# Graph attention with Strassen products on one core: side tasks split at each wait and spaced, the head weights folded with a on TensorE, the last feed-forward steps held as filler

## The chip, the core and the metric

One core of a Trainium2 chip runs the kernel. The metric is device time in microseconds of one execution, the median of several runs. The engines are PE (matmuls and transposes; its weight load PEld overlaps), DVE, ACT, POOL, and SP, which here only issues DMAs.

## The reference, cut to what matters

x is (128, 64, 512) in float32: 128 graphs of 64 nodes that share one adjacency matrix.

```python
h = jnp.maximum(_layernorm(x, axis=-1), 0.0)
def _gat_heads(x, adj, W, a):
    Wh = jnp.einsum('bnf,hfo->bhno', x, W)
    f1 = jnp.einsum('bhno,ho->bhn', Wh, a[:, :O])
    f2 = jnp.einsum('bhno,ho->bhn', Wh, a[:, O:])
    e = f1[:, :, :, None] + f2[:, :, None, :]
    e = jnp.where(e > 0, e, LEAKY_ALPHA * e)
    e = jnp.where(adj[None, None] > 0, e, NEG_INF)
    attn = jax.nn.softmax(e, axis=-1)
    return jnp.einsum('bhnm,bhmo->bhno', attn, Wh)
h = jax.nn.elu(_gat_heads(h, adj, W_heads, a_heads))      # 4 heads
h = jnp.transpose(h, (0, 2, 1, 3)).reshape(B, N, -1)      # 2048 wide
out = jax.nn.elu(_gat_heads(h, adj, W_out[None], a_out[None])[:, 0])
ffn = jnp.maximum(out @ w1 + b1, 0.0) @ w2 + b2
y = ffn + out
x + (y - mu) / jnp.sqrt(var + LN_EPS) * ln_gamma + ln_beta
```

## The kernel before

The 8192 rows are 64 tiles of 128 rows (two graphs each). Four tiles are a group, and there are 16 groups. Five stages make a group's work.

**Stage a** (L374) reads x, normalizes it (`norm1`, L273: BN_STATS on DVE L264, one small power on POOL, `n1nb` on DVE L278, the ReLU to `hn` on ACT L280), transposes `hn` on PE (`pth`, L293), copies it on ACT (`hT`, L295), and multiplies it with the 8 columns of `wa`, the head weights folded with a (`pf`, L300). Softmax 1 (L306, for a pair of tiles) spreads f2 over the diagonal of an identity (`s1dg`, DVE L311), lets PE add it up over the rows (`s1pe`, L318), then adds, masks, takes leaky ReLU, exponential (`s1e`, ACT L329), sum, reciprocal and `s1A` (DVE L343). PE transposes the weights (`s1pt`, L360 to L368) and ACT copies them to `at`.

**attend1** (L396) multiplies the attention weights with `hn` itself, ahead of the head projection (`pz` into `z`). **project1** (`g_a`) multiplies z with the head weights, one head at a time, and `late` work on ACT, DVE and POOL applies elu and forms the sums `hS`, `h` (L434, L435, L472, L499). **project2** (`g_b`) multiplies the 2048-wide result with W_out and gives `wh` (L505, L507).

**Stage e** (L543) is the second attention: the scores `jf` (eight on DVE, L522), `s2dg`, `s2pe`, `s2A`, the transposes `s2pt` (L532), and `pa` (attend2, L538) with elu to `o`. **feed_forward** (L551) transposes `o` (`pto`, L561, to `ot`), does the two products `g_c` and `g_d` with the ReLU `rt` between (ACT L588), and `finish` normalizes (`n2st`, L264; L607, L608), adds x (`xr`) and stores.

Each product of a group with a 512 by 512 weight is done in Strassen-Winograd form: seven products p of 256-wide quadrants in place of eight (`unit`, L182). Sums and differences of the quadrants of the activations are made on POOL or DVE (`sums`, L252 to L255: `zs_z`, `zs_o`, `hS`), those of the results on ACT and DVE (`s_a`, `t_a`, L193, L195). The p-th result goes to one of three banks of the unit, so that the order of p says when each sum is needed. The sums of weights are made once at the start by POOL (`weight_sums`, L139), stored to DRAM (`tc`), and every piece is then streamed from DRAM by SP through a ring of 12 buffers `w` (`piece`, L154).

Order of the work (L624 to L678): in iteration g, project1(g), 24 steps of g_a, carries a side list of stage_e(g-1) (stage_a(1) for g=0), whose entries are spread evenly over the steps. project2(g), 28 steps of g_b, carries attend1(g+1), the transposes, the two products and finish of feed_forward(g-1), and stage_a(g+2). `mix` interleaves lists by their fractions and `run` spreads a side list over steps. An entry that does nothing (`lambda: None`) is a gap. A scheduler then places the instructions on the in-order queue of each engine, so that an instruction that has to wait holds all behind it on its engine. PSUM is six banks for products and two ("aux") for transposes, scores and spreads.

At the start, ACT issues the loads of the weights (`fetch`, buffers `pw`); `fold` (L124) multiplies the head weights with a row of a, broadcast to all rows (`ab`), in 32 DVE operations with accumulation (`jk`, L133); and POOL's weight sums wait for the last of these by a dependency made by hand.

Of the kernel before, what the change touches and what calls it, by code (L numbers as in the profile page):

```python
# [20 lines left out]
def gat_preln_kernel(  # L21
# [38 lines left out]
    G = 4  # L60
# [63 lines left out]
    def fold(m):  # L124

        for c in range(2):
            ab = wk.tile([P, O], FP, tag="elu", name=f"ab{c}_{m}", bufs=3)
            nc.sync.dma_start(
                out=ab, in_=a_heads[m:m + 1, c * O:(c + 1) * O].to_broadcast([P, O])
            )  # L130
            for k in range(KC):
                junk = wk.tile([P, O], FP, tag="t", name=f"jk{c}_{m}_{k}")
                last = nc.vector.scalar_tensor_tensor(  # L133
                    junk, MT[m][:, k, :], 1.0, ab, ALU.mult, ALU.mult,
                    accum_out=wa[:, k, c * H + m:c * H + m + 1],
                )
        return last

    def weight_sums(m):  # L139
# [5 lines left out]
        first = nc.gpsimd.tensor_tensor(s[0][:, 0], b12, b11, ALU.subtract)  # L145
# [6 lines left out]
        return first  # L152
# [133 lines left out]

    def project_f(p):

        hts = []
        for t in (2 * p, 2 * p + 1):  # L290
            pt = aux([P, KC, P], f"pth{t}")
            for k in range(KC):
                nc.tensor.transpose(pt[:, k, :], HN[t][:, ts(k, P)], ident)  # L293
            hT = wk.tile([P, KC, P], FP, tag="hT", name=f"hT{t}")
            nc.scalar.copy(hT, pt)  # L295
            hts.append(hT)
        pf = aux([P, 2, 2 * H], f"pf{p}")
        for j, hT in enumerate(hts):
# [7 lines left out]
    def softmax(f1, f2, q, tag, t):  # L306
# [9 lines left out]
        )  # L316
        pe = aux([P, q, N], f"{tag}pe{t}")
# [15 lines left out]
        nc.vector.reciprocal(r, s)  # L333

# [17 lines left out]

    def attn_weights(p):
        f = FF.pop(p)
        A1[p] = softmax(
            f[:, 0].rearrange("p t h -> p (t h)"), f[:, 1].rearrange("p t h -> p (t h)"),
            2 * H, "s1", p,
        )

    def transpose_weights(p):  # L360
        A = A1.pop(p)
        for j in range(2):
            t = 2 * p + j
            pt = aux([P, H, P], f"s1pt{t}")
            for h in range(H):
                nc.tensor.transpose(pt[:, h, :], A[:, j * H + h].rearrange("p b m -> p (b m)"), ident)
            AT[t] = big.tile([P, H, P], FP, tag="at", name=f"at{t}", bufs=G)
            nc.scalar.copy(AT[t], pt)  # L368
# [255 lines left out]
    for m in range(H):  # L624
        fetch(m)
# [84 lines left out]
```

## Time and profile before

| what | value |
|---|---|
| median of 3 runs | 2600.03 us (2592.85 to 2607.5) |
| the profiled execution's own time | 2600.03 us |
| its span, first to last instruction | 2598.2 us |
| PE busy | 2408.9 us, 93% |
| DVE / ACT / POOL busy | 1495.3 / 775.1 / 1002.8 us |
| mean granted TensorE clock | 0.970 |
| DMA | 371.03 MB, 143 GB/s in the mean |

PE is busy nearly all the time, so the table is read for the rest: what PE waits for, where it runs at a lower clock, and what the first and last hundred microseconds hold in which it is not yet, or no longer, fully fed. One iteration of the loop takes 157.0 us in the middle of the run.

### The profile page before, as it was taken

The page shows a single profiled execution, that of the slowest core. Times are in us where ns is not written, and L with a number is a line of the kernel's source. Part 1 is how long each engine was busy: PE and PEld are TensorE (multiplying, and loading weights), DVE is VectorE, ACT ScalarE, POOL GpSimd, SP SyncE. Part 2 cuts the span into 40 slices and gives each one's busy share as a digit, 9 for nine tenths or more (in the row PEclk, how much of TensorE's full clock was granted, in tenths as well). Part 3 has the DMA queues.
Part 4 walks back from the last instruction along what each step waited for, and adds up shares of the span by engine and source line. Part 5 has one row for each costly group of instructions (what it writes and reads, how often), then busy time and mean ns, then how long its engine had stood idle before and what let it go on. Part 6 is the DMA issues. An engine that isn't in the chain of part 4 may idle for free.

```text
span 2598.2 us, 32561 instructions
## 1 busy us (share of the span) xinstructions
PE 2408.9 (93%) x11552; PEld 2012.8 (77%) x11552; DVE 1495.3 (58%) x2566; ACT 775.1 (30%) x1345; POOL 1002.8 (39%) x851
## 2 busy tenths in 40 slices
PE   1599999999999999999999999999999999899995
PEld 1488787788788887888788788887887878788884
DVE  6565556474654747557465654747556473744645
ACT  0242414224142331414224151331514223141401
POOL 5733422434334343432534333343432434333342
PEclk9899999999999999999999999999999999999998
DMA  8643434344443444435344443444444354434451
GB/s 288 218 130 126 133 124 156 114 159 133 142 135 120 158 132 146 133 120 165 122 159 133 155 131 115 157 133 150 131 129 158 123 161 130 150 125 151 151 165 50
DMA packets 261584, 371.03 MB, mean 143 GB/s; under 512 B 22448, under 2 KB 145328, under 8 KB 261424
## 3 DMA queue, kind: packets, MB, share of 16 engines
q1 hardware_dynamic: 253264, 347.99, 42.0%
q10 hardware_dynamic: 5280, 10.49, 1.2%
q0 software_dynamic: 2880, 10.49, 1.0%
q8 instruction: 93, 1.52, 0.2%
q14 instruction: 67, 0.55, 0.1%
HBM read 341.61 MB, written 27.26 MB: 142 GB/s over the span
## 4 chain that ended last, share of the span: by engine, by line
PE 77%; DVE 15%; issue 3%; DMA 2%; POOL 1%; ACT 1%; SPq 0%; DVEq 0%; POOLq 0%; ACTq 0%
PE g_a L228 27%; PE g_b L243 23%; PE g_d L243 7%; PE g_c L228 6%; PE pz L411 4%; PE pf L300 2%; DVE o L608 2%; DVE jf L522 2%; PE pa L538 2%; PE pzS L411 1%; PE pto L561 1%; DVE s1A L343 1%; DVE n2st L264 1%; PE s1pe L318 1%; DVE o L607 1%
## 5 line engine op out<-in xcount | busy, mean ns | idle before, releaser
L243 PE MATMUL g_b<-w,h 128*128 128x256 f32 x2560 | 603.4, 381 | 0.0
L243 PEld LDWEIGHTS g_b<-w,h 128*128 128x128 f32 x2560 | 477.4, 190 | 78.2 <-issue 14.0
L228 PE MATMUL g_a<-zs_z,w 128*128 128x256 f32 x1536 | 367.6, 388 | 14.5 <-POOL zs_z L253 12.9
L228 PE MATMUL g_a<-z,w 128*128 128x256 f32 x1536 | 374.9, 386 | 0.0
L228 PEld LDWEIGHTS g_a<-zs_z,w 128*128 128x128 f32 x1536 | 299.8, 196 | 65.0 <-POOL zs_z L253 13.3
L228 PEld LDWEIGHTS g_a<-z,w 128*128 128x128 f32 x1536 | 296.8, 193 | 48.9 <-issue 4.4
L243 PE MATMUL g_b<-w,hS 128*128 128x256 f32 x1024 | 264.6, 397 | 0.0
L472 POOL TENSOR_TENSOR hS<-hS,h 128x512 f32<-128x512 f32 x64 | 81.3, 1271 | 401.3 <-DVE hS L435 401.3
L243 PEld LDWEIGHTS g_b<-w,hS 128*128 128x128 f32 x1024 | 190.6, 195 | 41.0 <-issue 11.4
L499 POOL TENSOR_TENSOR h<-h,h 128x512 f32<-128x512 f32 x64 | 85.4, 1336 | 252.3 <-PE g_b L243 252.3
L434 ACT ACTIVATE exc<-exc 128x512 f32<-128x512 f32 x256 | 161.4, 630 | 7.6
L253 POOL TENSOR_TENSOR zs_z<-zS,z 128x512 f32<-128x512 f32 x64 | 89.8, 1404 | 151.4 <-PE g_d L243 83.2
L255 POOL TENSOR_TENSOR zs_z<-z,zs_z 128x512 f32<-128x512 f32 x64 | 81.8, 1278 | 162.4 <-PE g_a L228 145.4
L435 DVE SCALAR_TENSOR_TENSOR h<-exc,h 128x512 f32<-128x512 f32 x128 | 105.7, 831 | 60.2 <-ACT exc L434 60.2
L243 PE MATMUL g_d<-w,rt 128*128 128x256 f32 x512 | 136.5, 415 | 0.7 <-ACT s_d L193 0.7
L243 PEld LDWEIGHTS g_d<-w,rt 128*128 128x128 f32 x512 | 106.5, 210 | 26.1 <-issue 6.2
L499 POOL TENSOR_TENSOR h<-hS,h 128x512 f32<-128x512 f32 x64 | 81.7, 1277 | 108.4 <-PE g_b L243 107.6
L228 PE MATMUL g_c<-ot,w 128*128 128x256 f32 x512 | 121.8, 381 | 0.0
L228 PE MATMUL g_a<-zS,w 128*128 128x256 f32 x512 | 121.1, 379 | 0.0
L599 POOL TENSOR_TENSOR o<-s_d,o 128x512 f32<-128x512 f32 x32 | 41.4, 1294 | 201.6 <-ACT s_d L193 160.0
L588 ACT ACTIVATE rt<-rt,b1s 128x256 f32<-128x256 f32 x96 | 43.5, 500 | 243.0 <-DVE rt L585 243.0
L604 POOL TENSOR_TENSOR xr<-xr,bs 128x512 f32<-128x512 f32 x64 | 85.5, 1337 | 74.3 <-DMA xr<-in_x_dram 51.9
(134 smaller groups left out, 3829.0 us busy)
## 6 DMA issues: line engine op xcount, KB each, us to landing
w<-tc SPq DMA_DIRECT2D x640, 256.0 KB, 2.7
w<-in_L_gnn_W_heads_dram SPq DMA_DIRECT2D x192, 256.0 KB, 2.8
w<-in_L_gnn_W_out_dram SPq DMA_DIRECT2D x192, 256.0 KB, 2.7
w<-in_L_gnn_w_dram SPq DMA_DIRECT2D x96, 256.0 KB, 2.7
x<-in_x_dram SPq DMA_DIRECT2D x66, 256.0 KB, 3.2
xr<-in_x_dram SPq DMA_DIRECT2D x64, 256.0 KB, 3.0
out_dram<-o SPq DMA_DIRECT2D x64, 256.0 KB, 2.2
tc<-pt POOLq DMA_DIRECT2D x20, 512.0 KB, 5.5
```

The costliest lines, as they stand in the source:

```text
L228: nc.tensor.matmul(bk[:, o, :], w[:, k, ts(o, P)], a[:, k, :], start=start and o == 0 and k == 0, stop=k == 1, skip_group_check=True,)
L243: nc.tensor.matmul(bk[:, j, :], a[:, k, ts(j, P)], w[:, k, :], start=start and k == 0 and j == 0, stop=i == len(ms) - 1 and k == 1, skip_g ...
L253: eng.tensor_tensor(s2, s1, a11, ALU.subtract)
L255: eng.tensor_tensor(s3, a22, s2, ALU.subtract)
L300: nc.tensor.matmul(pf[:, j, :], hT[:, k, :], wa[:, k, :], start=(k == 0), stop=(k == KC - 1))
L411: nc.tensor.matmul(banks[b][:, c, :].rearrange("p (h n) -> p h n", h=H), src[rows, off + c * P:off + (c + 1) * P], at[rows, :, rows], star ...
L434: nc.scalar.activation(ex, ex, AF.Exp, scale=-1.0)
L435: nc.vector.scalar_tensor_tensor(dst, ex, -1.0, src, ALU.add, ALU.max)
L472: nc.gpsimd.tensor_tensor(dst, dst, H1["22"][:, h], ALU.add)
L499: nc.gpsimd.tensor_tensor(dst[:, h], x0[:, h], x1[:, h], ALU.subtract)
L522: nc.vector.scalar_tensor_tensor(junk, WH2[g][:, j], 1.0, ao[:, c, :], ALU.mult, ALU.mult, accum_out=f[:, c, j:j + 1],)
L604: nc.gpsimd.tensor_tensor(xr, xr, bs, ALU.add)
```

## The change

Six edits are made.

1. `fold` moves from DVE to PE. a is loaded once (`ah`, 16 KB, in place of eight broadcasts) and transposed; each of the 16 blocks of 128 rows of the head weights is transposed in four parts (`pwt`), copied from PSUM by ACT or DVE in turn (`wT`), and multiplied with two columns of a (`pwa`). POOL's weight sums no longer wait for the fold. The startup runs norms, transposes of hn, fold, then per pair scores and softmax, then the transposes of the weights.
2. The side tasks are split where one engine waits for another: `transpose_h` from `project_f` (with four `hT` buffers in place of two), `spread` from `softmax`, and the scores from softmax 2. stage_a has 15 entries in place of 9 and stage_e 25 in place of 24, with gaps between.
3. The weights of softmax 1 are 512 elements (e times r, heads side by side and the first repeated) in place of a block-diagonal 1024, and `at` is laid out per graph.
4. The order of p in g_d is (1, 6, 5, 2, 3, 7, 4) in place of (1, 2, 6, 5, 7, 3, 4).
5. The first z sums (group 0, head 0) go to DVE in place of POOL.
6. In the last iteration the last seven steps of g_d of group 14 are held out of project2(15) and run with the first 15 entries of stage_e(15). The last feed_forward puts two finishes after step 12 of 14.

```diff
-                last = nc.vector.scalar_tensor_tensor(
-                    junk, MT[m][:, k, :], 1.0, ab, ALU.mult, ALU.mult,
-                    accum_out=wa[:, k, c * H + m:c * H + m + 1],
-                )
+    def fold(m, aT, pw):
+        for k in range(KC):
+            pt = bank(f"pwt{m}_{k}").rearrange("p a b -> p (a b)").rearrange("p (o q) -> p o q", o=KC)
+            for o in range(KC):
+                nc.tensor.transpose(pt[:, o, :], MT[m][:, k, ts(o, P)], ident)
+            wT = wk.tile([P, KC, P], FP, tag="elu", name=f"wT{m}_{k}", bufs=3)
+            if k % 2 == 0:
+                nc.scalar.copy(wT, pt)
+            else:
+                nc.vector.tensor_copy(wT, pt)
+            for o in range(KC):
+                nc.tensor.matmul(
+                    pw[:, k, :, m], wT[:, o, :], aT[:, m, :, o],
...
+    def transpose_h(t):
+        pt = aux([P, KC, P], f"pth{t}")
...
+        HT[t] = wk.tile([P, KC, P], FP, tag="hT", name=f"hT{t}", bufs=4)
+        nc.scalar.copy(HT[t], pt)
...
         return [
-            lambda: norms(p), lambda: project_f(p), lambda: norms(r), lambda: attn_weights(p),
-            lambda: project_f(r), lambda: transpose_weights(p), lambda: attn_weights(r),
+            lambda: norms(p), lambda: norms(r), lambda: transposes(p), lambda: transposes(r),
+            lambda: f(p), lambda: None, lambda: attn_weights(p), lambda: f(r), lambda: None,
+            lambda: attn_weights(r), lambda: None, lambda: transpose_weights(p), lambda: None,
             lambda: None, lambda: transpose_weights(r),
         ]
...
+        eng = nc.vector if (g, h) == (0, 0) else nc.gpsimd
+        sums(eng, z["S1"][:, h], z["11"][:, h], z["12"][:, h], z["22"][:, h], *ZSUM[h])
...
-        return [lambda: softmax2(g)] + wait * 9 + [lambda: transpose_weights2(g)] + wait + [
-            lambda: (attend2(g, 0), attend2(g, 1))] + wait + [lambda: (attend2(g, 2), attend2(g, 3))
-        ] + wait * 8
+            [lambda: scores2(g)] + gap * 6 + [lambda: softmax2(g)] + gap * 6
+            + [lambda: transpose_weights2(g)] + gap * 2 + attend[0:1] + attend[1:2] + gap
+            + attend[2:3] + attend[3:4] + gap * 3
...
-        tail = mix(ff, stage_a(g + 2)) if ff or g + 2 < NG else []
-        run(project2(g), mix(attn, tr) + tail + fin if attn or tr else tail + fin)
-    for fn in stage_e(NG - 1):
+        if g < NG - 1:
...
+        else:
+            held = len(ff) - 7
+            run(project2(g), tr + [lambda: None] * 8 + ff[:held])
+            run(ff[held:] + fin, stage_e(g)[:15])
+    for fn in stage_e(NG - 1)[15:]:
         fn()
-    for fns in feed_forward(NG - 1):
-        run(fns)
+    tr, ff, fin = feed_forward(NG - 1)
+    run(tr + ff[:12] + fin[:2] + ff[12:] + fin[2:])
```

**First place: the head of project1.** PE's queue at the first steps of project1 of group 2, before. `g_a` are the products of head 0 (bank 0) in the order of p that the number in `w` tells, and `s2pe` is the spread of softmax 2 of group 1.

```order
L228 MATMUL g_a_0_2546<-z_2_1882,w_1_2547 128x256 x4
L228 MATMUL g_a_0_2592<-zs_z_0_2540,w_6_2593 128x256 x4
L228 MATMUL g_a_0_2601<-zS_2_1962,w_5_2602 128x256 x4
L228 MATMUL g_a_0_2546<-z_2_1905,w_2_2616 128x256
L318 MATMUL s2pe_2574<-s2dg_2572,blkones 128x256
L228 MATMUL g_a_0_2546<-z_2_1905,w_2_2616 128x256 x3
L228 MATMUL g_a_0_2592<-zs_z_0_2541,w_7_2626 128x256 x4
L228 MATMUL g_a_0_2601<-zs_z_0_2542,w_3_2637 128x256 x4
```

PE after, from the same product on:

```order
L240 MATMUL g_a_0_2642<-z_2_1980,w_1_2643 128x256 x4
L240 MATMUL g_a_0_2670<-zs_z_0_2636,w_6_2671 128x256 x4
L240 MATMUL g_a_0_2679<-zS_2_2053,w_5_2680 128x256 x4
L240 MATMUL g_a_0_2642<-z_2_2003,w_2_2694 128x256 x4
L240 MATMUL g_a_0_2670<-zs_z_0_2637,w_7_2704 128x256 x4
L240 MATMUL g_a_0_2679<-zs_z_0_2638,w_3_2715 128x256 x4
L240 MATMUL g_a_1_2726<-z_2_1980,w_1_2727 128x256 x4
L341 MATMUL s2pe_2735<-s2dg_2668,blkones 128x256
L240 MATMUL g_a_1_2753<-zs_z_1_2688,w_6_2754 128x256 x4
L240 MATMUL g_a_0_2670<-z_2_2077,w_4_2762 128x256 x4
```

`s2pe` stood in the middle of the fourth product and now stands after the seventh, behind the whole of head 0's p=1, 6, 5, 2, 7, 3 and the first product of head 1.

DVE's queue at the same place, before: the end of `wh`, the scores `jf` and the spread `s2dg`, and the sums `t_a` and `s_a` of project1's first results; `n1st` are statistics of x for a later group.

```order
L507 TENSOR_TENSOR wh_2_2917<-g_b_3085,s_b_2984 128x2x256
L608 SCALAR_TENSOR_TENSOR o_2743<-o_2743,n2rs_3574,xr_3565 128x512
L522 SCALAR_TENSOR_TENSOR jf_2_0_3607,f_2_3598<-wh_2_2917,ao 128x512
L522 SCALAR_TENSOR_TENSOR jf_2_1_3609,f_2_3598<-wh_2_2917,ao 128x512
L522 SCALAR_TENSOR_TENSOR jf_3_0_3611,f_2_3598<-wh_2_2917,ao 128x512
L522 SCALAR_TENSOR_TENSOR jf_3_1_3613,f_2_3598<-wh_2_2917,ao 128x512
L195 TENSOR_TENSOR t_a_0_3642<-g_a_0_3635,s_a_0_3596 128x512
L311 TENSOR_TENSOR s2dg_3615<-eye,f_2_3598 128x256
L264 BN_STATS n1st_4251<-x_4174 128x6
L195 TENSOR_TENSOR s_a_0_3651<-g_a_0_3644,s_a_0_3596 128x512
L323 TENSOR_TENSOR s2e_3619<-s2pe_3617,f_2_3598 128x256
```

DVE after, from the same `wh` on:

```order
L550 TENSOR_TENSOR wh_2_3013<-g_b_3209,s_b_3080 128x2x256
L565 SCALAR_TENSOR_TENSOR jf_2_0_3701,f_2_3692<-wh_2_3013,ao 128x512
L565 SCALAR_TENSOR_TENSOR jf_2_1_3703,f_2_3692<-wh_2_3013,ao 128x512
L565 SCALAR_TENSOR_TENSOR jf_3_0_3705,f_2_3692<-wh_2_3013,ao 128x512
L565 SCALAR_TENSOR_TENSOR jf_3_1_3707,f_2_3692<-wh_2_3013,ao 128x512
L327 TENSOR_TENSOR s2dg_3709<-eye,f_2_3692 128x256
L207 TENSOR_TENSOR t_a_0_3718<-g_a_0_3711,s_a_0_3690 128x512
L276 BN_STATS n1st_4266<-x_4246 128x6
L278 BN_AGGR n1mv_4268<-n1st_4266 128x2
L280 TENSOR_SCALAR n1ve_4270<-n1mv_4268 128x1
L207 TENSOR_TENSOR s_a_0_3727<-g_a_0_3720,s_a_0_3690 128x512
L276 BN_STATS n1st_4280<-x_4248 128x6
```

`s2dg` now stands ahead of `t_a`, and `s_a` stands behind the statistics, their mean and variance (`n1mv`, `n1ve`) of one tile of x.

**Second place: the transposes of hn in project2.** PE's queue in project2 of group 1, before; `pth` are the transposes for a pair of tiles and `pf` the product that needs their copy `hT`.

```order
L243 MATMUL g_b_2042<-w_7_2274,hS_1_1495 128x256 x4
L293 MATMUL pth_2280<-ident,hn_2175 128x128 x4
L293 MATMUL pth_2287<-ident,hn_2189 128x128 x4
L243 MATMUL g_b_2042<-w_7_2305,hS_1_1495 128x256 x2
L300 MATMUL pf_2294<-wa,hT_2285 128x8 x4
L243 MATMUL g_b_2042<-w_7_2305,hS_1_1495 128x256
L300 MATMUL pf_2294<-wa,hT_2292 128x8 x4
L243 MATMUL g_b_2042<-w_7_2305,hS_1_1495 128x256
L243 MATMUL g_d_2311<-w_1_2312,rt_0_2104 128x256 x4
```

PE after, around the transposes and the first `pf` of the same stage:

```order
L304 MATMUL pth_2232<-ident,hn_2150 128x128 x4
L304 MATMUL pth_2239<-ident,hn_2162 128x128 x4
L255 MATMUL g_b_2168<-w_6_2246,h_1_1591 128x256 x4
L240 MATMUL g_c_2252<-zs_o_2113,w_6_2253 128x256 x4
L255 MATMUL g_b_2168<-w_6_2261,h_1_1591 128x256 x4
L304 MATMUL pth_2269<-ident,hn_2194 128x128 x4
L304 MATMUL pth_2276<-ident,hn_2208 128x128 x4
L240 MATMUL g_c_2283<-ot_0_2069,w_5_2284 128x256 x4
L255 MATMUL g_b_1973<-w_2_2292,h_1_1592 128x256 x4
L314 MATMUL pf_2298<-wa,hT_2237 128x8 x4
L314 MATMUL pf_2298<-wa,hT_2244 128x8 x4
```

Between the transposes and the `pf` that reads them stood two of g_b's four matmuls; now five products of four matmuls and the other pair's transposes stand there.

ACT's queue at the same place, before, with the activations `rt` of the feed-forward:

```order
L588 ACTIVATE rt_0_2105<-rt_0_2105,b1s 128x256 x2
L505 COPY wh_1_1874<-g_b_1875 128x2x256
L329 ACTIVATE s1e_2222<-s1e_2222 128x512
L588 ACTIVATE rt_0_2104<-rt_0_2104,b1s 128x256 x2
L588 ACTIVATE rt_0_2105<-rt_0_2105,b1s 128x256 x2
L295 COPY hT_2285<-pth_2280 128x512
L295 COPY hT_2292<-pth_2287 128x512
```

ACT after, around the same copies:

```order
L292 ACTIVATE hn_2208<-x_2166,n1nb_2206,n1rs_2204 128x512
L205 COPY s_c_2182<-g_c_2175 128x512
L638 ACTIVATE rt_0_2228<-g_c_2175,b1s 128x256 x2
L306 COPY hT_2237<-pth_2232 128x512
L306 COPY hT_2244<-pth_2239 128x512
L306 COPY hT_2274<-pth_2269 128x512
L306 COPY hT_2281<-pth_2276 128x512
L638 ACTIVATE rt_0_2229<-rt_0_2229,b1s 128x256 x2
L638 ACTIVATE rt_0_2228<-rt_0_2228,b1s 128x256 x2
```

The copies `hT` stood behind all four `rt` activations of the feed-forward and an exponential; now all four stand behind one `rt` and ahead of the other three.

**Third place: the startup on ACT.** ACT's queue before, from the seventh weight load on (`pw` in turn: heads 0 to 3, W_out in four parts, w1, w2):

```order
L122 DMA pw_437<-in_L_gnn_W_out_dram 128x4x512
L295 COPY hT_300<-pth_295 128x512
L329 ACTIVATE s1e_272<-s1e_272 128x512
L122 DMA pw_425<-in_L_gnn_W_out_dram 128x4x512
L368 COPY at_318<-s1pt_313 128x512
L368 COPY at_325<-s1pt_320 128x512
L421 COPY z_0_473<-pz_0_0_474 128x2x4x64
L421 COPY z_0_482<-pz_0_0_483 128x2x4x64
L122 DMA pw_449<-in_L_gnn_w_dram 128x4x512
L329 ACTIVATE s1e_331<-s1e_331 128x512
L122 DMA pw_461<-in_L_gnn_w_dram 128x4x512
```

ACT after, from the first copy of the fold on:

```order
L143 COPY wT_2_225<-pwt_2_220 128x512
L122 DMA pw_503<-in_L_gnn_W_out_dram 128x4x512
L306 COPY hT_195<-pth_190 128x512
L143 COPY wT_0_247<-pwt_0_242 128x512
L143 COPY wT_2_269<-pwt_2_264 128x512
L143 COPY wT_0_291<-pwt_0_286 128x512
L143 COPY wT_2_313<-pwt_2_308 128x512
L143 COPY wT_0_335<-pwt_0_330 128x512
L143 COPY wT_2_357<-pwt_2_352 128x512
L122 DMA pw_515<-in_L_gnn_W_out_dram 128x4x512
L122 DMA pw_527<-in_L_gnn_W_out_dram 128x4x512
L122 DMA pw_539<-in_L_gnn_W_out_dram 128x4x512
```

The sixth load, `pw_515`, is now issued behind the fold's last ACT copy, where before `pw_437`, the seventh, was issued behind three copies of `hT` and the sixth behind none.

## Prediction on record

> **What bounds the kernel now.** I read the page first, for the busy shares of the engines.
>
> ```profile
> span 2598.2 us, 32561 instructions
> PE 2408.9 (93%) x11552; PEld 2012.8 (77%) x11552; DVE 1495.3 (58%) x2566; ACT 775.1 (30%) x1345; POOL 1002.8 (39%) x851
> ```
>
> PE is the bound: it is busy for 93% of the span, and the next engine for 58%. The change makes hardly any of PE's work smaller, so what it can win is the time in which PE idles or runs at a lower clock. For this I took PE's busy time over the steady stretch (126 to 2534 us), and in two short windows that lie at the two waits of one group. The columns are the window, its length, the busy time of PE, PEld, DVE, ACT and POOL with counts, then the granted clock.
>
> ```profile
> 126.00:2534.00 2408.00, 2330.41 (x11214) 1952.78 (x11212) 1385.19 (x2353) 742.17 (x1289) 902.90 (x749) 0.98 0.44 139
> 511.00:519.00 8.00, 7.94 (x29) 6.93 (x30) 3.12 (x6) 0.50 (x2) 0.00 (x0) 0.57 0.11 35
> 558.00:564.00 6.00, 5.65 (x19) 4.71 (x20) 5.04 (x15) 1.65 (x3) 0.13 (x1) 0.72 0.45 162
> ```
>
> In the steady stretch PE idles 2408.0 - 2330.4 = 77.6 us. The clock of 0.98 costs another 0.02 x 2408 = 48 us; as 0.98 stands for 0.975 to 0.985, that is 36 to 60. The third view, PE's waits by what ended them in this stretch (sum, times, longest), has only two rows:
>
> ```profile
> PE s2pe L318 <- DVE s2dg L311: 50.6, 15, 4.5
> PE pf L300 <- ACT hT L295: 27.0, 13, 2.1
> ```
>
> 50.6 + 27.0 = 77.6, so these two waits are all of the idle time. The two short windows stand right behind one wait of each kind: in 8 us at 0.57, 3.4 us of clock are lost, in 6 us at 0.72, 1.7. So the lost clock follows the waits. 13 x 3.4 + 15 x 1.7 = 70 is more than the 48 that there is, so not every group pays as much as this one; I go by the 48.
>
> **The spread of softmax 2 (change 2).** T0 is the start of project1, 549.19 in the group shown. PE's timeline:
>
> ```profile
> 549.19 1.89 PE L228 MATMUL g_a<-z,w 128*128 128x256 f32 x8
> ...
> 554.37 0.59 PE L228 MATMUL g_a<-z,w 128*128 128x256 f32 x2
> 558.35 0.67 PE L318 MATMUL s2pe<-s2dg,blkones 128*128 128x256 f32 x2 [3.38 <-DVE s2dg L311]
> ```
>
> (The profile counts two records a matmul.) From the first product of z to the fourth, (554.37 - 549.19) / 3 = 1.73 us a product. `s2pe` was placed inside the fourth, at T0+5.8, and waited 3.38 us. It now stands behind seven products, at T0 + 7 x 1.73 = T0+12.1. DVE's queue decides whether `s2dg` is there by then:
>
> ```profile
> 541.48 0.74 DVE L607 SCALAR_TENSOR_TENSOR o<-o,n2mv,gs 128x512 f32<-128x512 f32 x1
> ...
> 542.87 1.41 DVE L608 SCALAR_TENSOR_TENSOR o<-o,n2rs,xr 128x512 f32<-128x512 f32 x2
> ...
> 544.80 0.69 DVE L599 TENSOR_TENSOR o<-g_d,o 128x512 f32<-128x512 f32 x1
> ...
> 546.01 1.28 DVE L264 BATCH_NORM_STATS2 n2st<-o 128x6 f32<-128x512 f32 x2
> ...
> 552.55 0.68 DVE L507 TENSOR_TENSOR wh<-g_b,s_b 128x512 f32<-128x512 f32 x1
> ...
> 554.74 0.68 DVE L522 SCALAR_TENSOR_TENSOR jf<-wh,ao 128x512 f32<-128x512 f32 x1
> ...
> 557.79 0.41 DVE L311 TENSOR_TENSOR s2dg<-eye,f 128x256 f32<-128x256 f32 x1
> 558.12 0.68 DVE L264 BATCH_NORM_STATS2 n1st<-x 128x6 f32<-128x512 f32 x1
> 558.72 0.67 DVE L195 TENSOR_TENSOR s_a<-g_a,s_a 128x512 f32<-128x512 f32 x1
> ```
>
> Even if `wh` comes as late as now (T0+3.36) and one more pair of finish passes (1.41) stands ahead of it, `s2dg` ends by T0 + 3.36 + 1.41 + 0.68 + 4 x 0.68 + 0.41 = T0+8.6, 3.5 us before PE asks. So 50.6 us of idle time go. By the new queue I expect earlier: from the first `wh`, which g_b's product p=3 releases some ten us before T0, DVE has 2 `wh`, 8 `jf`, 2 `o` sums, 4 L608, 2 L607, 2 statistics and `s2dg`, which is 14 us at these rows, so `s2dg` ends at T0+4.5 to 5.2.
>
> What is late next? PE writes p=7 and p=3, the fifth and sixth products, into banks that `t_a` and `s_a` must have read first: at T0 + 4 x 1.73 = 6.9 and T0 + 5 x 1.73 = 8.65. `t_a`, right behind `s2dg`, ends at 5.1 to 5.8, in time. `s_a` stands behind `n1st` of a tile of x, and that waits for a load that SP issues behind the stores of finish:
>
> ```profile
> 552.84 0.40 SPq L93 DMA_DIRECT2D x<-in_x_dram  x1
> ...
> 556.30 0.42 SPq L93 DMA_DIRECT2D x<-in_x_dram  x1
> ```
> ```profile
> 560.57 0.69 DVE L264 BATCH_NORM_STATS2 n1st<-x 128x6 f32<-128x512 f32 x1 [0.32 <-DMA x<-in_x_dram]
> ```
> ```profile
> x<-in_x_dram SPq DMA_DIRECT2D x66, 256.0 KB, 3.2
> ```
>
> The first load is issued at T0+3.65 now; with the stores some tenths earlier I take T0+2.6 to 3.6. A load lands after 3.2 us (median), or after 560.57 - 556.30 = 4.3 as here. Then `n1st` takes 0.68, two small operations some 0.3, `s_a` 0.67: it ends at T0+7.4 to T0+9.5, beside 8.65. The wait is 0 to 0.9 us, taken as 0.45: 15 x 0.45 = 7 us.
>
> **The transposes of hn (change 2).** PE and ACT in project2:
>
> ```profile
> 507.08 1.04 PE L293 MATMUL pth<-ident,hn 128*128 128x128 f32 x8
> ...
> 511.06 1.21 PE L300 MATMUL pf<-wa,hT 128*128 128x8 f32 x8 [2.08 <-ACT hT L295]
> ```
> ```profile
> 509.63 0.91 ACT L588 ACTIVATE rt<-rt,b1s 128x256 f32<-128x256 f32 x2 [3.89 <-DVE rt L585]
> 510.45 1.05 ACT L295 COPY hT<-pth 128x512 f32<-128x512 f32 x2
> ```
>
> The copy `hT` was ready to run at 508, but stood behind an `rt` that waited 3.89 us for DVE. Now the copies stand ahead of those activations, and five products and a pair of transposes lie between transpose and `pf`: 5 x 1.73 + 1.0 = 9.7 us, against 1.05 for two copies. So 27.0 us go. The `rt` activations come up to 4 x 0.53 = 2.1 us later behind four copies, and g_d, which reads them, stands some products on; so I cost that at nothing. If that cover were gone it would cost at most 2.1 x 13 = 27 us.
>
> **The clock.** With no wait left in the steady stretch, the 48 us go (36 to 60). Here the profile can be read in two ways, since pf and transposes are small matmuls, too. In the startup:
>
> ```profile
> 43.34 1.94 PE L293 MATMUL pth<-ident,hn 128*128 128x128 f32 x8 [43.34 <-POOL pt L146]
> ...
> 63.08 1.77 PE L300 MATMUL pf<-wa,hT 128*128 128x8 f32 x8
> 66.17 1.88 PE L300 MATMUL pf<-wa,hT 128*128 128x8 f32 x8 [1.32 <-ACT hT L295]
> ```
> ```profile
> 119.11 1.03 PE L300 MATMUL pf<-wa,hT 128*128 128x8 f32 x8
> ```
>
> A pass of pf takes 1.77 / 8 = 0.22 us at half clock and 1.03 / 8 = 0.129 at full. That a wait of 2.08 us is followed by 0.57 speaks for the wait as cause, but pf itself stands there as well. By the Trainium skill ("TensorE: Matmul & The Clock Gate", section "HAM oscillation - how this bites in real kernels") only idle gaps of more than about 3.4 us lower the clock, which speaks against the pf wait as the cause; the trace, with 0.57 after a wait of 2.08, doesn't bear that out as it stands, and by the page these groups' loss would stay (a rival below).
>
> **Smaller edits of the steady groups (3, 4).** Smaller `s1A` work, other strides of `s1pt` and g_d's order are on DVE and PE's side work. DVE has 42% free, and PE has as many transposes as before. I cost them at nothing; their cover is that no row of the waits names them.
>
> **The startup (1, 5).** The chain of waits up to the first p=6 product, which waits for POOL's first z sum:
>
> ```profile
> 38.02 2.54 DVE jk L133 x9
> 40.63 5.08 DMA pw<-in_L_gnn_W_out_dram
> ...
> 70.39 9.96 DMA pw<-in_L_gnn_W_out_dram
> ...
> 87.31 8.80 DMA pw<-in_L_gnn_w_dram
> 96.25 1.26 POOL pt L145
> ...
> 106.62 1.81 DVE n1nb L278 x2
> ```
> ```profile
> 112.69 3.56 PE L228 MATMUL g_a<-zs_z,w 128*128 128x256 f32 x8 [12.94 <-POOL zs_z L253]
> ```
>
> Before, DVE's fold ends at 40.6. After, PE does 64 transposes at 1.94 / 8 = 0.24 and 64 matmuls in two passes at 0.22 from about 13 us on, with the 16 transposes `pth` ahead: 15.5 + 28.2 + 3.9 = 48, end at about 61 to 64. ACT issues the sixth weight load behind the last copy, at about 58. From there each buffer is loaded (10) and summed (4 x 1.26 = 5) twice, 88, and the last load (8.8) lands at 97 to 99. Behind it three POOL sums (3.8) and the powers (1.1), then, as now, 112.69 - 106.62 = 6.1 us, less a POOL sum (1.3) plus one on DVE (0.6), and up to 2 less if DVE has less queued: p=6 starts at 107 to 109 in place of 112.7. I take -4. Bounds: +12, if the 16 copies aren't hidden (16 x 0.53 = 8.5) and the loads meet; -26 with a warm PE (a rival).
>
> **The end (6).** Of the last iteration's PE timeline, and its last spread:
>
> ```profile
> 2523.50 10.52 PE L243 MATMUL g_b<-w,h 128*128 128x256 f32 x48
> ...
> 2544.98 1.12 PE L532 MATMUL s2pt<-ident,s2A 128*128 128x128 f32 x4 [5.44 <-DVE s2A L343]
> ```
>
> g_b ends at 2534.0 and `s2pt` comes 11.0 later. With seven g_d products held out, g_b ends 7 x 1.73 = 12.1 earlier, and the held ones fill the wait on PE. But DVE's work on them (4 L607, 4 L608, 4 statistics, 4 `o` sums: 3.0 + 2.8 + 2.6 + 2.8 = 11.2) now stands between the last `wh` and `s2A`, so `s2pt` comes only 12.1 - 11.2 = 1 us earlier. Two finishes put ahead of the end take about 3 us (0.74 + 0.70 each, with statistics) off it: -4 (-10 if DVE fits them into its waits, +6 if the finishes hold `s2A`).
>
> **The sum.** -50.6 - 27.0 - 48 + 7 - 4 - 4 = -126.6. 2598.2 - 126.6 = 2471.6. The profiled execution's own time is 2600.03, 1.8 above its span and equal to the median of the runs shown; so 2473.
>
> **Rivals.** (a) The wait moves to `s_a`: each group idles 2 us at p=3 and loses 1.7 of clock as behind `s2pe`. 15 x 3.7 = 55.5 in place of 7: 2473 + 48.5 = 2522. For it: `n1st` already waits for its load. Against it: 8.65 lies well inside 7.4 to 9.5. 12%, and 3 points of this lie within 13 us of the present time.
>
> (b) PE warms up in the fold, as it has 128 passes and 64 transposes on end: 64 x 0.13 + 128 x 0.129 = 24.8 in place of 43.7, some 19 us earlier, and the weight loads with it: 2454. Against it: pf at 66.17 still takes 0.23 a pass though PE had been at transposes and pf since 59.34. 18%. The Trainium skill, same page, section "What's actually happening", lets about 3.4 us of activity release the clock, which is for it, and Part 4 says that transposes don't count, which is against.
>
> (c) The loss of clock at pf is from pf and transposes, not from the wait: of the 48, 44 / 70 stay (30 us): 2503. For it: the small matmuls at half clock above; against it: at 119.11 they run at full clock. 10%.
>
> (d) Slower than before: `n1st` blocks DVE's queue ahead of `s_a` for long, as its load stands on SP's queue behind stores that wait for finish. At 9.9 us a group (149 / 15, idle and clock together) it passes 2613; for that the load must land at about T0+15, in place of 7. At 11 us a group: 2473 - 7 + 165 = 2631. 4%. That the waits are as before because the scheduler leaves `s2pe` where it was is excluded by the queue shown.
>
> **How the numbers follow.** Forecast 56%, (a) 12, (b) 18, (c) 10, (d) 4. A measurement of this kernel can tell about 0.5%, 13 us. Faster: 56 + 9 + 18 + 10 = 93%; same 3; slower 4. The range: down, warm PE (-19), the most clock (-12), no `s_a` wait (-7), the end at -10 (-6): 2429. Up, (a) with the startup at its far end (+12 in place of -4, less what doesn't fall together, 6): 2532.
>
> **What would show it.** In the profile after, the rows `s2pe` <- `s2dg` and `pf` <- `hT` are gone from PE's waits, the steady stretch's clock is 0.99 or 1.00 and it is about 119 us shorter; any row left is `g_a` <- DVE `s_a`. p=6 starts at 107 to 109, after a fold at 0.22 a pass. I am wrong if the clock stays at 0.98 with the waits gone (c), or if a row with DVE or a load as releaser has over 30 us (a).

## The result, and the profile after

The changed kernel takes 2442.18 us in the median of four runs (2441.74 to 2449.17), the kernel before 2596.44 beside it: a ratio of 0.9407, 95% interval 0.937 to 0.9444. The profiled execution is the slowest of the four, 2449.17 us with a span of 2447.4. So the traces account for 2598.2 - 2447.4 = 150.8 us of the 154.3 between the medians; the changed kernel's other three executions are some 7 us shorter than the profiled one, and that of before lies 3.6 above its median; no trace shows where.

The page of the changed kernel:

```profile
span 2447.4 us, 32886 instructions
PE 2382.2 (97%) x11745; PEld 2020.3 (83%) x11745; DVE 1446.5 (59%) x2515; ACT 770.9 (31%) x1353; POOL 1006.6 (41%) x848
```

I cut both traces at the same two places: the start of the first p=6 product of g_a and the last g_a. Up to the first, before took 112.7 us and after 104.2 (-8.5). From there to the last g_a lies the steady stretch; its rows, first of before and then of after:

```profile
112.69:2459.40 2346.71, 2267.54 (x10918) 1897.34 (x10919) 1356.52 (x2313) 734.41 (x1274) 878.69 (x734) 0.98 0.44 139
```
```profile
104.16:2310.80 2206.64, 2199.86 (x10917) 1867.27 (x10918) 1337.09 (x2315) 725.47 (x1274) 886.40 (x731) 1.00 0.46 147
```

2346.71 - 2206.64 = 140.1 us are won here, and 2.2 in what is left. Idle time falls from 79.2 to 6.8, and PE's busy time by 67.7, with the clock at 1.00. The throttle's records in the trace hold 20 stretches at half clock that begin in this part before (105.8 us, so 52.9 lost), the last 3.2 us of one that began in the startup (1.6 lost), and one stretch of 3.4 us after (1.7 lost): 52.8 of the 67.7 are clock. Of the 52.9, 22.2 belong to the 11 stretches that begin 8 to 12 us after a T0, behind the wait of s2pe (T0 is the start of a group's project1), and 30.7 to nine that follow pf. PE's waits in the stretch, after:

```profile
PE g_a L240 <- issue: 5.3, 3, 3.2
PE g_a L240 <- DVE s_a L207: 1.5, 2, 1.3
PE g_a L240 <- DVE t_a L207: 1.4, 1, 1.4
```

Neither s2pe nor pf is there any more. (1.45 us of the first row lie just ahead of the stretch.) At the head of project1 in iteration g=3, the one that the prediction showed (T0 is now 518.93), first PE's timeline, then DVE's:

```profile
518.93 1.89 PE L240 MATMUL g_a<-z,w 128*128 128x256 f32 x8
...
531.02 0.59 PE L341 MATMUL s2pe<-s2dg,blkones 128*128 128x256 f32 x2
```
```profile
519.13 0.69 DVE L550 TENSOR_TENSOR wh<-g_b,s_b 128x512 f32<-128x512 f32 x1 [0.55 <-PE g_b L255]
...
522.43 0.42 DVE L327 TENSOR_TENSOR s2dg<-eye,f 128x256 f32<-128x256 f32 x1
522.77 0.68 DVE L207 TENSOR_TENSOR t_a<-g_a,s_a 128x512 f32<-128x512 f32 x1
524.10 0.69 DVE L276 BATCH_NORM_STATS2 n1st<-x 128x6 f32<-128x512 f32 x1 [0.64 <-DMA x<-in_x_dram]
...
525.11 0.68 DVE L207 TENSOR_TENSOR s_a<-g_a,s_a 128x512 f32<-128x512 f32 x1
```

s2pe is asked for at T0+12.1, as forecast. More telling is `wh`: it waited 0.55 us for PE, so DVE had nothing left to do when g_b ended. Before, the same `wh` came at T0+3.36 out of a full queue. s2dg now ends at T0+3.9, t_a at 4.5 and s_a at 6.9, all ahead of PE. Why DVE is free there is the question of most of the experiments.

### The profile page after: what moved, and what is told of

Same layout as the page of the kernel before. It is cut to its first block, busy times and chain, and to the rows that moved or that the text cites. A ratio compares the mean times of both kernels' runs of the same rounds, so it can differ in the third digit from the quotient of the medians.

```text
span 2447.4 us, 32886 instructions
## 1 busy us (share of the span) xinstructions
PE 2382.2 (97%) x11745; PEld 2020.3 (83%) x11745; DVE 1446.5 (59%) x2515; ACT 770.9 (31%) x1353; POOL 1006.6 (41%) x848
## 4 chain that ended last, share of the span: by engine, by line
PE 93%; DVE 3%; DMA 2%; issue 1%; POOL 1%; ACT 0%; SPq 0%; DVEq 0%; ACTq 0%; POOLq 0%
PE g_b L255 31%; PE g_a L240 31%; PE g_c L240 8%; PE g_d L255 7%; PE pz L453 4%; PE pf L314 2%; PE pa L585 2%; DMA x<-in_x_dram 1%; PE pzS L453 1%; PE pto L611 1%; PE s1pe L341 1%; PE pth L304 1%; PE s1pt L399 1%; PE pwa L147 1%; DVE o L658 0%
## 5 line engine op out<-in xcount | busy, mean ns | idle before, releaser
L240 PE MATMUL g_a<-zs_z,w 128*128 128x256 f32 x1536 | 357.9, 381 | 8.2 <-issue 5.3
L240 PE MATMUL g_a<-z,w 128*128 128x256 f32 x1536 | 363.0, 379 | 0.0
L240 PEld LDWEIGHTS g_a<-zs_z,w 128*128 128x128 f32 x1536 | 292.2, 191 | 57.3 <-issue 14.5
L240 PEld LDWEIGHTS g_a<-z,w 128*128 128x128 f32 x1536 | 291.6, 190 | 53.1 <-issue 15.2
L255 PE MATMUL g_b<-w,hS 128*128 128x256 f32 x1024 | 244.8, 385 | 0.0
L255 PE MATMUL g_d<-w,rt 128*128 128x256 f32 x512 | 122.2, 382 | 2.4 <-DVE n2ve L280 1.1
L267 POOL TENSOR_TENSOR zs_z<-z,zs_z 128x512 f32<-128x512 f32 x63 | 89.8, 1426 | 84.1 <-PE g_a L240 70.1
L475 ACT ACTIVATE exc<-h 128x512 f32<-128x512 f32 x128 | 80.6, 629 | 130.1 <-DVE h L512 130.1
L266 POOL TENSOR_TENSOR zs_z<-z,zs_z 128x512 f32<-128x512 f32 x63 | 80.6, 1280 | 80.5 <-PE g_d L255 63.7
L240 PEld LDWEIGHTS g_a<-zS,w 128*128 128x128 f32 x512 | 96.1, 190 | 18.8 <-issue 7.2
L255 PEld LDWEIGHTS g_d<-w,rt 128*128 128x128 f32 x512 | 96.0, 190 | 16.0 <-DVE n2ve L280 1.5
```

The lines of the kernel that those rows point to most:

```text
L240: nc.tensor.matmul(bk[:, o, :], w[:, k, ts(o, P)], a[:, k, :], start=start and o == 0 and k == 0, stop=k == 1, skip_group_check=True,)
L255: nc.tensor.matmul(bk[:, j, :], a[:, k, ts(j, P)], w[:, k, :], start=start and k == 0 and j == 0, stop=i == len(ms) - 1 and k == 1, skip_g ...
L266: eng.tensor_tensor(s4, a12, s2, ALU.subtract)
L267: eng.tensor_tensor(s3, a22, s2, ALU.subtract)
L475: nc.scalar.activation(ex, src, AF.Relu, scale=-1.0)
```

## The experiments

"Steady" below is the stretch between the two cuts in the run's own profile, to the end of the last g_a; "half-clock loss" is half of the time at half clock in it; "s2dg" is its end after T0, the median of the 15 groups.

| run | median us | steady | idle in it | half-clock loss | s2dg |
|---|---|---|---|---|---|
| before | 2596.4 | 2347.1 | 79.2 | 54.5 | T0+9.05 |
| order of p alone | 2609.8 | 2356.0 | 78.8 | 65.5 | T0+7.20 |
| stage e split alone | 2572.3 | 2321.3 | 60.4 | 44.7 | T0+9.19 |
| stage a split alone | 2540.0 | 2288.4 | 56.8 | 33.4 | T0+9.69 |
| changed, old order of p | 2495.0 | 2247.6 | 35.6 | 10.2 | T0+9.69 |
| changed, stage a joined | 2489.9 | 2250.8 | 22.6 | 13.7 | T0+7.24 |
| changed, spread early | 2460.8 | 2215.4 | 9.7 | 5.1 | T0+3.92 |
| changed | 2442.2 | 2207.0 | 6.8 | 1.7 | T0+3.92 |

For the steady stretch the eight rows are the eight combinations of three edits: the order of p, the split of stage e, the split of stage a. (Change 3 and the four `hT` buffers go with the split of stage a, but stay in the row "stage a joined".) The order of p costs 9 us alone and saves 73 beside the split of stage a (2288.4 to 2215.4) and 41 beside both splits (2247.6 to 2207.0).

**The spread early again.**

```diff
-            [lambda: scores2(g)] + gap * 6 + [lambda: softmax2(g)] + gap * 6
-            + [lambda: transpose_weights2(g)] + gap * 2 + attend[0:1] + ...
+            [lambda: (scores2(g), softmax2(g))] + gap * 9 + [lambda: transpose_weights2(g)] + gap
+            + [lambda: (attend2(g, 0), attend2(g, 1))] + ...
```

> The changed kernel with the list of stage e of before: scores, spread and softmax 2 start together at the first step, so s2pe stands in PE's queue in the third product of project1 (about T0+3.9 us, T0 the start of project1) and no longer behind the seventh; DVE's queue keeps the changed kernel's order (last finish passes, wh, jf, s2dg, t_a). Theory A (the split alone took the wait away): the 50.6 us of idle time and 25 us of clock come back, about 2517 us. Theory B (the new order of DVE's queue took most of it, since in the changed kernel's trace s2dg ends at 522.85, T0+3.9, where in the kernel before it ended at T0+9.0): PE asks at T0+3.9 and waits 0.2 to 1 us a group, 3 to 15 us in all, and the clock falls little: 2445 to 2465 us.

2460.83 us (2458.11 to 2464.59). The wait came back in three groups only:

```profile
PE s2pe L341 <- DVE s2dg L327: 9.4, 3, 4.0
```

From 20 us ahead of T0 to t_a, DVE's queue is instruction for instruction that of the changed kernel, and s2dg ends at T0+3.92 again, just ahead of PE, which asks at T0+4.05. So theory B holds: of the 73 us that s2pe's wait (50.6) and the half clock behind it (22.2) cost before, the place of s2pe accounts for little once DVE is free. The 19 us of the median are 8.3 in the steady stretch, 3.4 in the startup, which is the same in both kernels, and 1 at the end by the profiles; the rest is the spread between executions that the result names.

**Transposes joined with pf again** (the nine entries of the old list).

```diff
-            lambda: norms(p), lambda: norms(r), lambda: transposes(p), lambda: transposes(r),
-            lambda: f(p), lambda: None, lambda: attn_weights(p), lambda: f(r), lambda: None,
+            lambda: norms(p), lambda: (transposes(p), project_f(p)), lambda: norms(r),
+            lambda: (spread1(p), attn_weights(p)), lambda: (transposes(r), project_f(r)),
...
```

> The changed kernel with stage a joined again as in the kernel before (transposes of hn, their copies and pf in one entry; nine entries). By the theory the waits of pf for hT come back, about 27 us (two pairs a group, 1 to 2 us each), and behind each the clock falls to a half for one or two windows of 3.4 us: about 3.4 us a group, 45 us at most. Theory: 2442 + 27 + 25 to 45 = 2494 to 2515 us, clock 0.98. Rival (the clock is not lowered by waits as short as 2 us): 2442 + 27 = 2469 us with the clock of the steady part at 1.00.

2489.89 us (2488.35 to 2495.91). PE's waits, and one of them with its window of 9 us:

```profile
PE g_a L240 <- issue: 10.8, 13, 1.5
PE pf L314 <- ACT hT L306: 9.7, 13, 0.8
```
```profile
343.93 1.06 PE L314 MATMUL pf<-wa,hT 128*128 128x8 f32 x8 [0.75 <-ACT hT L306]
```
```profile
341.00:350.00 9.00, 8.25 (x41) 7.02 (x40) 5.63 (x9) 1.86 (x4) 2.00 (x2) 0.76 0.21 60
```

The waits are smaller than forecast (9.7 and 10.8, not 27), yet seven stretches at half clock came with them, each behind a wait at pf, with no idle piece over 1.7 us in the steady stretch. So the rival (short waits leave the clock alone) falls for pf. A new wait at g_a stands beside it: with the softmax late again, s2dg ends at T0+7.24 and t_a behind it. These waits last up to 1.7 us, longer than those at pf, and no stretch at half clock follows any of them.

**The fold on DVE** (change 1 undone, the rest of the startup kept).

> The changed kernel with the fold of the head weights on DVE again, POOL's sums behind it as before, and the rest of the startup kept (all transposes of hn, then scores and softmax). In the trace the first product with p=6 starts at 104.2 in the changed kernel and at 112.7 in the kernel before. If the fold on PE brought this, it goes back to about 110 to 115: 2450 us. If the new order of the startup and the z sum on DVE brought it and the fold on PE, at half clock from 28 to 64 us, is itself the brake, p=6 starts earlier, at 85 to 95, and the time is 2425 to 2433 us.

2457.12 us (2451.93 to 2458.52). The first p=6 product:

```profile
113.55 3.75 PE L228 MATMUL g_a<-zs_z,w 128*128 128x256 f32 x8 [9.94 <-issue]
```

113.55 against 104.16: the first theory, 9.4 us. The larger difference of the medians (15) again holds the 7 us of the result. The startup itself varies: in the seven profiles with the changed kernel's startup p=6 starts at 102.4 to 108.4, in the three with that of before at 112.7 to 113.5.

**The end as before** (change 6 undone).

> The changed kernel with the last iteration and the last feed-forward in the order of the kernel before (nothing held out of project2, no finishes interleaved). From the start of the last g_b to the end the traces take 139.0 us before and 136.4 after, so by the prediction's step the end is worth 2 to 4 us: 2444 to 2446 us. Rival: the held steps fill the 10 us of waits, and without them 2450 us or more.

2448.23 us (2446.09 to 2449.98), 6 more in the median, which lies between the two forecasts; by the profiles 137.1 us from the last g_a to the end against 136.2, which speaks for the small value.

**Each part alone, and the change without the order of p.** Stage e alone on the kernel before:

> The kernel before with one part of the change alone: the scores and the spread of stage e split from softmax 2, and its entries spaced as in the changed kernel. s2pe now stands behind the seventh product, but DVE's queue at the head of project1 stays that of the kernel before (a finish pass between wh and jf; t_a ended at T0+8.6 there). Prediction's step: the 50.6 us of idle time at s2pe go, and 25 us of clock: about 2520 us. Rival (a), in this kernel: PE asks for p=7 at T0+6.9, t_a ends at T0+8.6, so 1.7 us of the wait stay there in each group (25 us in all, named t_a or s_a), with clock lost: 2545 to 2570 us.

2572.27 us, ratio 0.9887 (0.9853 to 0.9921). s2pe waits no more, but

```profile
PE g_a L228 <- issue: 29.9, 22, 2.8
PE pf L300 <- ACT hT L295: 26.9, 13, 2.1
```

the wait went to g_a. The profile names no releaser, but in each of the 14 groups that wait at p=7 the product starts 0.10 us behind the end of t_a (T0+8.6 to 9.8). Rival (a) is what happens here, only at p=7, one product sooner than the prediction put it. Stage a alone (with change 3):

> The kernel before with the split and spaced stage a, and the smaller weights of softmax 1 (without them four hT buffers do not fit). s2pe stays inside the fourth product (T0+5.6). If the wait at s2pe is a matter of its place alone, this takes away only the 27 us at pf and the clock behind it (20 to 45): 2525 to 2550 us. If the earlier softmax 1 is what lets DVE come to s2dg in time (as the run with the spread early made likely: with s2pe asked for at T0+3.5 its wait came back in 3 of 15 groups only), most of the s2pe wait goes as well: 2455 to 2480 us.

2540.03 us, ratio 0.9773 (0.9746 to 0.98). The first reading holds, and my theory of the earlier softmax falls:

```profile
PE s2pe L329 <- DVE s2dg L315: 52.6, 13, 4.1
```

DVE is idle for 6.7 us in the last 20 before T0 (1.7 before), but not at all in the last 10. Then the changed kernel with one line undone:

```diff
-        f2 = unit(f"d{g}", ..., post2, (1, 6, 5, 2, 3, 7, 4))
+        f2 = unit(f"d{g}", ..., post2, (1, 2, 6, 5, 7, 3, 4))
```

> The changed kernel with the order of p in g_d of before. By the prediction it is worth nothing: 2442 us, within 8. Rival: it is what moved the finishes of two tiles ahead, and with it back DVE reaches s2dg and s_a later: waits at g_a for t_a or s_a of 1 us a group, 2455 us or more.

(In this kernel the two finishes that the last feed-forward puts ahead of its end run before p=3 has been added to their tiles, so for those two tiles of the last group the sum is incomplete; every other group does its whole work.) 2495.04 us (2491.94 to 2496.91): 53 us for an edit that the prediction costed at nothing, 41 of them in the steady stretch. Waits, PE's timeline and DVE's at T0 = 524.21:

```profile
PE g_a L240 <- issue: 34.2, 16, 2.4
```
```profile
533.61 3.69 PE L240 MATMUL g_a<-zs_z,w 128*128 128x256 f32 x16 [2.33 <-issue]
```
```profile
523.43 0.73 DVE L657 SCALAR_TENSOR_TENSOR o<-o,n2mv,gs 128x512 f32<-128x512 f32 x1
...
524.36 0.74 DVE L657 SCALAR_TENSOR_TENSOR o<-o,n2mv,gs 128x512 f32<-128x512 f32 x1
...
526.26 0.75 DVE L658 SCALAR_TENSOR_TENSOR o<-o,n2rs,xr 128x512 f32<-128x512 f32 x1 [1.16 <-POOL xr L654]
526.93 0.68 DVE L550 TENSOR_TENSOR wh<-g_b,s_b 128x512 f32<-128x512 f32 x1
...
530.55 1.74 DVE L658 SCALAR_TENSOR_TENSOR o<-o,n2rs,xr 128x512 f32<-128x512 f32 x1
...
532.82 0.68 DVE L207 TENSOR_TENSOR t_a<-g_a,s_a 128x512 f32<-128x512 f32 x1
533.43 0.41 DVE L327 TENSOR_TENSOR s2dg<-eye,f 128x256 f32<-128x256 f32 x1
```

The product p=7 starts at 533.61, just behind t_a (ends 533.50); the profile names no releaser for it, but the 0.10 us between them are the same in all 14 groups that wait. With p=3 sixth of the seven products of g_d, all four finishes come after it, and two of their last passes (L658) lie behind T0. With p=3 fifth, tiles 0 and 1 are whole one product sooner (5.2 us, as other products stand between), and their half of the finish work falls into time in which DVE idles. In the changed kernel, 14.4 us ahead of T0:

```profile
504.51 0.69 DVE L649 TENSOR_TENSOR o<-g_d,o 128x512 f32<-128x512 f32 x1 [0.85 <-PE g_d L255]
...
508.70 1.40 DVE L658 SCALAR_TENSOR_TENSOR o<-o,n2rs,xr 128x512 f32<-128x512 f32 x2
```

One more thing stretches DVE's queue in the run with the old order: a `jf` (528.87) and the last L658 take 1.75 and 1.74 us in place of 0.69 and 0.74, each beside a tensor operation of POOL. They are 2.1 of the 5.8 us by which s2dg ends later than in the changed kernel.

Is that edit then enough by itself?

> The kernel before with change 4 alone: the order of p in g_d (1, 6, 5, 2, 3, 7, 4). Between the first g_a with p=6 and the last g_a the profiles have 2347.1 us before, 2288.4 with stage a alone, 2215.4 with stage a and the order of p (s2pe early), so the order was worth 73 us there. Theory (two tiles finish two products sooner, DVE is through with its finish passes before project1 starts, and s2dg comes in time even for an early s2pe): the same 60 to 75 us without the split, s2pe's wait below 15 us, pf's wait of 27 us unchanged: about 2525 to 2540 us. Rival (it works only together with the earlier softmax 1): under 25 us, 2575 us or more.

2609.82 us, ratio 1.0055 (1.0039 to 1.007): slower, if anything. The theory falls, and the rival (only together, 2575 us or more) holds.

```profile
PE s2pe L318 <- DVE s2dg L311: 46.1, 14, 3.9
PE pf L300 <- ACT hT L295: 26.9, 13, 2.1
```

Here the finishes are ready sooner, but DVE is at softmax 1 and its queue stays full (1.2 us idle in the last 20 before T0, which is 547.61):

```profile
531.31 0.69 DVE L328 TENSOR_TENSOR s1e<-s1e,s1mx 128x512 f32<-128x512 f32 x1
...
535.36 1.21 DVE L343 TENSOR_TENSOR s1A<-s1e,s1rb 128x1024 f32<-128x1024 f32 x1
...
549.33 1.40 DVE L608 SCALAR_TENSOR_TENSOR o<-o,n2rs,xr 128x512 f32<-128x512 f32 x2
```

s2dg ends at T0+7.20, and the scheduler put s2pe in the third product, so it waits as before. The table's last column is the explanation: with the old softmax or the old order DVE carries a backlog across T0 (7.2 to 9.7); with both moved it has none (3.92), as it then starts from `wh`, and that from PE. The order alone takes 1.9 us off the 9.05, the split of stage a alone nothing; the two together take 5.1.

**Small matmuls together.** pf of the first pair right behind the transposes of the second.

```diff
-            lambda: norms(p), lambda: norms(r), lambda: transposes(p), lambda: transposes(r),
-            lambda: f(p), lambda: None, lambda
+            lambda: norms(p), lambda: norms(r), lambda: transposes(p), lambda: None,
+            lambda: None, lambda: (transposes(r), f(p)), lambda
```

> The changed kernel with pf of the first pair put right behind the transposes of the second pair (one matmul of g_b between), so that about 2.7 us of transposes and 8-column matmuls stand together while PE waits for nothing. If the clock falls because such work counts little (the rival (c) of the prediction), half-clock windows of 3.4 us come back in about half of the groups or more: 2442 + 12 to 45 us. If it falls because of the wait, nothing changes: 2442 us, clock of the steady part 1.00.

2443.97 us (2443.28 to 2451.88). One cluster, and its window:

```profile
471.25 1.04 PE L304 MATMUL pth<-ident,hn 128*128 128x128 f32 x8
...
472.55 1.92 PE L314 MATMUL pf<-wa,hT 128*128 128x8 f32 x16
```
```profile
471.00:475.00 4.00, 4.00 (x31) 3.64 (x31) 1.15 (x3) 1.86 (x4) 0.03 (x1) 1.00 0.36 120
```

There is no stretch at half clock between the cuts at all. Small matmuls without a wait did not lower the clock; rival (c), which needs no wait, falls.

**The fold shared, and the end.** Two versions that the profiles pointed to. Heads 0 and 1 folded on PE, 2 and 3 on DVE:

> The changed kernel with heads 0 and 1 folded on PE and heads 2 and 3 on DVE as before (16 operations of 0.6 us, beside PE). In the changed kernel PE is at the fold from 28 to 64 us at 0.21 us a pass, and the first product of project1 starts at 100.7, p=6 at 104.2. If the fold on PE bounds the startup, half of it takes 20 us off: p=6 at about 84 to 90, about 2424 us. Rival: the loads and POOL's weight sums bound it (or DVE, which does the fold and the norms in one queue), and p=6 stays at 100 or later: 2440 us.

2440.48 us, ratio 0.9391 (0.936 to 0.9422), not to be told from the changed kernel. The p=6 product starts at 93.0, but PE waits for DVE on the way there and behind it:

```profile
45.81 1.86 PE L147 MATMUL pwa<-aT,wT 128*128 128x2 f32 x8 [7.65 <-DVE wT L145]
...
103.66 3.58 PE L254 MATMUL g_a<-zs_z,w 128*128 128x256 f32 x8 [4.43 <-DVE t_a L221]
```

Finishes of group 14 behind the last attention, with o of the last group in another buffer:

```diff
+            OUT[g] = big.tile([P, G, FO], FP, tag="out" if g < NG - 1 else "z11", name=f"o{g}")
...
-            run(ff[held:] + fin, stage_e(g)[:15])
+            run(ff[held:], stage_e(g)[:15])
+            last = fin
...
+    run(tr + ff[:5] + last + ff[5:12] + fin[:2] + ff[12:] + fin[2:])
```

> The changed kernel with the four finishes of group 14 put behind the attention of the last group, and o of the last group in a buffer of its own (that of z11), so that they have to end nowhere before it. In the changed kernel s2pt waits 6.4 us for s2A, behind DVE's finish work. If that work is what takes the gain of the held steps, s2A comes 4 to 8 us earlier and the end with it: 2435 to 2439 us. Rival: DVE's work only moves into the last feed-forward and delays its sums: 2442 us or more.

2436.64 us, ratio 0.9377 (0.9351 to 0.9402); from the last g_a to the end 128.9 us against 136.2. s2pt, which waited 6.39 us for s2A in the changed kernel, doesn't wait:

```profile
2394.70 1.11 PE L579 MATMUL s2pt<-ident,s2A 128*128 128x128 f32 x4 [6.39 <-DVE s2A L374]
```
```profile
2381.88 0.66 PE L579 MATMUL s2pt<-ident,s2A 128*128 128x128 f32 x4
```

So the finish work was what took the gain of the held steps. Both together, with all of the fold's copies on ACT:

> The run with the finishes behind the last attention, and the fold shared: heads 0 and 1 on PE with all eight copies on ACT, heads 2 and 3 on DVE. With the fold shared and half of its copies on DVE, p=6 started at 93.0 in place of 104.2, but PE waited 7.7 us for a copy behind DVE's fold, and the fourth sum of project1 came at 102.9, behind POOL's sums. If the copies are free of DVE, the fold ends some 10 us earlier (at about 47 in place of 59) and the first products with it: p=6 at 80 to 88, and 2436.6 - 8 to 18 = 2419 to 2429 us. Rival: the loads of W_out and POOL's sums bound the first head, PE waits there for what it has won, and the time is 2433 to 2437 us.

2433.65 us, ratio 0.9362 (0.9344 to 0.938). The rival's number: p=6 starts at 99.2, later than with the fold shared alone, as PE waits 13.5 us for DVE at the two softmaxes (8.4 there). It beats both kernels, but isn't told apart from the run before it.

## Why the prediction was right, and where its steps were not

The forecast was 2473 us in 2429 to 2532, and 2442 came; 24 us of the difference are in the traces. Term by term, from the sum to the measured profile:

- The waits at s2pe and pf: gone as forecast. The 7 us allowed for s_a came as 6.8 in all: 1.5 for s_a, 1.4 for t_a, and 3.9 in the last two groups, where the product starts 0.10 us behind t_a. In the group shown s_a ended at T0+6.9, ahead of 7.4. Idle time -72.4 in place of -70.6 (-50.6 - 27.0 + 7).
- The clock: -52.8 in place of -48. It went with the waits. The half clock returned with short waits among small matmuls (stage a joined) and not with small matmuls alone (put together).
- Startup: -8.5 in place of -4 (4 to 11 by the spread of the startups named above). The fold ended when it was forecast, PE going on to pf at 64.1 (61 to 64), with passes of 0.21 us, so rival (b), a warm PE, did not come:

```profile
58.70 5.12 PE L147 MATMUL pwa<-aT,wT 128*128 128x2 f32 x24
64.11 3.58 PE L314 MATMUL pf<-wa,hT 128*128 128x8 f32 x16 [0.29 <-DVE wa L684]
...
104.16 1.97 PE L240 MATMUL g_a<-zs_z,w 128*128 128x256 f32 x8 [1.45 <-issue]
```

But the path was another. The forecast ran over the last weight load (landed at 97 to 99) and POOL's sums. That load had landed by 93.3, when POOL took it up, and the profile's chain to the first products runs from the fold over softmax 1 on DVE and attend1 on PE; DVE's own z sum (change 5) ends 0.1 us ahead of p=6:

```profile
90.92 1.18 DVE s1A L363
...
93.47 3.72 PE pz L453 x16
...
100.78 1.94 PE g_a L240 x8
```

That 104.2 lies only 3 to 5 us from the 107 to 109 forecast is in part luck.

- The end: -2.2 in place of -4. s2pt came 1.7 us earlier, counted from the last g_a (1 was forecast), for the reason given; the finishes put ahead brought little.
- Not in the sum: 14.9 us of PE's busy time that is not clock. It goes with the split of stage a: busy time less half-clock loss is 2212 to 2216 in every run with the joined list and 2197 to 2202 in every run with the split one. Some 4 us of it are the drains of a matmul ahead of a wait (0.16 each, from 0.38 duration and 0.22 pitch; 29 waits before, 5 after). Another 6 lie at changes between products, which use 128 rows, and attend1, which uses 64: from a product's record to the first of `pz` or `pzS` it takes 0.31 us in place of 0.22, and from the last of these to a product or `pto` 0.31 in place of 0.11 (in the lines below 299.71 to 300.02, and 1.06 for the eight records of `pzS`). The split list lets `pzS` follow `pz` directly in 13 groups, and the stretch has 162 such changes in place of 214. The other 5 us stay open.

```profile
299.71 0.38 PE L255 MATMUL g_b<-w,hS 128*128 128x256 f32 x1
300.02 1.13 PE L453 MATMUL pzS<-at,hns 64*128 64x256 f32 x8
301.08 1.99 PE L255 MATMUL g_b<-w,hS 128*128 128x256 f32 x8
```

These lines are from the run with the small matmuls together; the pitches are the same in all runs. The terms make up the 150.8 us: 72.4 + 52.8 + 8.5 + 2.2 + 14.9.

The step that failed: "I cost them at nothing", on changes 3 and 4, covered by "no row of the waits names them". The order of p in g_d is worth 53 us in the changed kernel (41 in the steady stretch). Its absence is rival (a) at nearly full size: 34.2 us idle at g_a, 2495 us measured where (a) gave 2522, with t_a and not s_a as the sum that is late. The forecast did not suffer, since DVE's time at T0 was worked out on the new queue, in which this edit already was. But it credited the wrong edit. The wait at s2pe went because DVE's backlog went, and the later place of s2pe is worth 8 us of the steady stretch on top (19 in the medians). Change 3 was costed at nothing too; no run differs by it alone, as it makes room for the split of stage a, so its own share in time is open.

Rival (d) did not come: no wait for s_a was over 1.3 us. That the x load has to land at T0+15 to make it so was not tried.

## What to carry to other kernels

Where a waiting engine asks for the end of a queue, look first at what stands ahead in that queue and since when, not at where the request stands: moving the request only hands the wait to the next reader (30 of 51 us here). Such a backlog can hang on two edits at once: two that each leave most of it (0.98 and 1.01 in the ratio) together removed it here. And an edit is not free because no wait names it: ask whose work becomes ready earlier or later by it.

## What the runs showed of the hardware

**The clock.** All stretches at half clock in the throttle's records last a multiple of 3.41 us, but for the last of each trace, which its end cuts off. In the run with stage a joined, PE waits 0.75 us at pf in 13 groups, beside transposes and 8-column matmuls; seven of these waits are followed by a stretch at half clock (0.76 in the window shown). In the same trace 14 waits of 0.2 to 1.7 us at g_a, among products of 256 columns, are followed by none, and in the run with the small matmuls together 2.7 us of transposes and 8-column matmuls without a wait are followed by none. So in these traces neither the short wait nor the small matmuls brought the half clock alone, but both together did in about half of the groups. Waits of 2.2 to 2.4 us at g_a (old order of p) were followed by one in 6 of 14 groups.

In the startup PE was busy for 33.8 of the 36 us from 28 to 64 with transposes and 2-column matmuls and stayed at half clock (the records have 0.5 from 22.3 to 87.1), at 0.21 us a pass. The passes of pf, with 8 columns, take 0.21 us there too, and 0.107 later. Being busy with small matmuls did not bring the full clock, but at full clock did not lose it.

**DVE beside POOL.** Of the 128 passes `jf` of the changed kernel, the 98 that run beside no tensor operation of POOL of 0.9 us or more take at most 0.69 us. The 16 that start while such a one runs take 1.05 to 1.75, and each ends 0.55 us behind the end of POOL's operation. With the old order of p there are 39 of these.
